# A fourth result buffer, a reordered row of N and a VectorE subtraction in a conditioned residual kernel

## The chip, the cores and the metric

The kernel runs on one core of a Trainium2 chip. The metric is the device time of one execution in microseconds (us). The kernel before took 302.66 us as the median of three runs (299.89 to 302.8). Times inside an execution come from one profiled execution and count from its first instruction.

The core's engines have short names in the profile: PE is TensorE (matrix products; PEld its weight loads), DVE is VectorE (elementwise work of one or two tensors), ACT is ScalarE (copies, casts, functions), POOL is GpSimd (here it issues transfers and little else), SP is SyncE (issues transfers). Products are summed in PSUM, in banks of 128 partitions x 512 fp32 numbers. Everything else lies in SBUF.

## The reference

For each of 8 batches there are an x of 1024 x 512 and a row of condition of 512 numbers. Cut to what matters:

```python
ae  = layernorm(cond) * ln_g + ln_b
xw  = gelu(ae @ w1 + b1) @ w2 + b2            # 2 * 512 * 8 numbers a batch
a, t = split(xw)                               # each 512 x 8
x   = x + (x + x @ (base + a @ t.T))
ys  = cond / sqrt(512)
d   = rsqrt((ys * ys) @ (weight * weight) + 1e-8)
out = x + ((x * ys) @ weight) * d
```

Both layers are linear in x once the condition is known. So out = x P, with P = (2I + base + a t^T) N and N = I + diag(ys) weight diag(d), all 512 x 512 and different for each batch.

## The kernel before, in words

**Numbers.** An fp32 matrix is held as two parts of the type fp32r: an upper part, rounded by an ACT cast, and a lower part, the matrix minus its upper part, mostly by one DVE tensor_sub. A product takes three matmuls: upper times upper, upper times lower and lower times upper. In the names, an h marks an upper and an l a lower part: `nh`/`nl` for N, `ph`/`pl` for P, `sh`/`sl` and `th`/`tl` for sums of blocks. `xs[b, j]` holds both parts of a quarter of x of batch b, `[:, 0]` the upper, `[:, 1]` the lower.

**The setup (to about 80 us).** It computes the condition's network (bank `px` gathers the product with w2, whose 16 blocks are loaded one after another by `w2_group`), then Q = (2I + base) N for the first batches, and the two stacks a and t of low rank, from which each batch gets its term. Batches 2 and 3 are made together by `Pair(2)`, called `two`, which forms Q of both by seven block products instead of eight. For product p, `make_n(p)` makes two rows of blocks of N, `round(p)` forms the sum that the product needs and starts its cast to `nh`, `finish(p)` gives the lower part `nl`, and `unit()` runs half of a product on PE (`pp` in the profile). Inside `n_half` (L335) DVE runs a scalar_tensor_tensor for each of two rows (kk = 0, 1) and then an add of the identity's blocks.

The stack t is made by the generator `rank_t` (L454), one step for each `next(steps)`. The step at L485 multiplies by a selection on PE (bank `ps_t`) and has ACT cast the upper part (`work`). The next step takes the lower part, `st_t`, on DVE, and sends it to memory on POOL's queue (`kept_t`). A later step runs `stack` again for the second group of batches, into another bank `ps_t`. These banks come from `misc`, a PSUM pool with two buffers; the second `ps_t` gets the buffer of the first when `st_t` has read it.

The order of the setup is written out by hand: every DVE, ACT, SP and PE instruction there is pinned to program order. The lines around the change are L811 to L880. After the second `make_n` there, in this order: `round(6)`, two seeds of banks for batch 0 (`seed_first`), half a product, `finish(6)`, `round(3)`, the second stack of t, two w2 blocks, half a product, `round(7)`, the last w2 block, `with_bias(0)` (DVE writes `xab`; ACT casts it to `work`; DVE forms the remainder `work`), `finish(3)`, two halves of product 6, the first stack of a (`ps_a`) and `finish(7)`.

**The main loop (about 74 to 252 us).** 48 tiles of 128 rows of x, 8 for each of batches 0 to 5. `main(b, t)` sums 12 matmuls of 512 columns in a bank `po`; ACT copies it to `o` and issues the store. Between the tiles stand `load_x` (raw x by SP), `split_x` (L710, the parts of a quarter of x), the rank terms (`pr`, with `fa` and `ft` loaded on POOL's queue) and the pairs of later batches. Here DVE, ACT and POOL are not pinned: a planner sets their order from its own costs, mostly along the program; PE keeps the written order. The lower part of `xs[0, 3]`, the last quarter of x of batch 0, is made in another way than the rest: ACT writes minus the upper part there, and a transfer on POOL's queue adds x from memory onto it.

**The late halves (252 us to the end).** Batches 6 and 7 each have two halves of 512 rows. `Seven.part` (L985) does a half with seven block products, in the order 1, 5, 6, 2, 7, 3, 4, pinned again. Products 1, 6, 7 and 4 sum up in bank `sw`, 5 and 3 in `sz`, 2 in `sv`. In between, ACT and DVE take partial sums out of the banks into the two results of the half: `o1` (products 1, 6, 2, 3) and `o2` (5, 7, 4). A product that adds onto a bank waits until the sum before has been read. Each result is 128 x 1024 numbers; they share the tag `o2`, a set of three buffers. A result is stored when it is whole: o1 after product 3, o2 after product 4. The steps of `make_left` for the next half are done one by one between the products.

Of the kernel before, what the change touches and what calls it, by code (L numbers as in the profile page):

```python
# [7 lines left out]
F32 = mybir.dt.float32  # L8
F32R = mybir.dt.float32r
AF = mybir.ActivationFunctionType  # L10
ALU = mybir.AluOpType
# [3 lines left out]
P = 128  # L15
NB = 8
NT = 1024
D = 512
# [12 lines left out]
def cond_resid_kernel(ctx: ExitStack, tc: tile.TileContext, small, cond, condrows, consts,  # L31
# [10 lines left out]
    nc = tc.nc  # L42
# [21 lines left out]
    ve, se, sy = InOrder(nc.vector), InOrder(nc.scalar), InOrder(nc.sync)  # L64
# [99 lines left out]
    def newton_rsqrt(v, sd, shape, name):  # L164

        r = sp.tile(shape, F32, name=f"r_{name}")
        ve.reciprocal(r, sd)
        t = sp.tile(shape, F32, name=f"t_{name}")
        ve.tensor_mul(t, r, r)
        ve.tensor_mul(t, t, v)  # L170
        ve.tensor_scalar(t, t, -0.5, 1.5, ALU.mult, ALU.add)
        return r, t
# [12 lines left out]
    r, t = newton_rsqrt(ve_l, sd, [NB, 1], "l")  # L185
# [103 lines left out]
    r, t = newton_rsqrt(v, sv, [P, KC, NB], "d")  # L289
# [15 lines left out]
    def work_tile():  # L305
        turns[0] += 1
        return work[:, turns[0] % KC, :]
# [24 lines left out]
            d_all[b + i] = t[:, i, :]  # L332
            nc.gpsimd.dma_start(t[:, i, :], d_out[b + i:b + i + 1, :].to_broadcast([P, D]))

    def n_half(b, j):  # L335

        n = npool.tile([P, 2, D], F32, tag="n", name=f"n_{b}_{j}", bufs=4)
        for kk in range(2):
            k = 2 * j + kk
            ve.scalar_tensor_tensor(n[:, kk, :], w_sb[:, k, :], ysT[:, k, b:b + 1],  # L340
                                           d_all[b], ALU.mult, ALU.mult)
        blk = n.rearrange("p k (c i) -> p (k c) i", i=P)[:, 2 * j:2 * j + 6:5, :]
        ve.tensor_add(blk, blk, ident.unsqueeze(1).to_broadcast([P, 2, P]))
        return n
# [49 lines left out]
    def w2_group():  # L394
        h, r, k = todo.pop(0)
        t = big_tile(f"w2_{h}_{r}_{k}")
        sy.dma_start(t, w2[h, r, k])
        if len(todo) == 15:
            sy.dma_start(cst, consts)
        if len(todo) == 8:  # L400
            sy.dma_start(crow, condrows)
            sy.dma_start(b2r, b2rows)
        if len(todo) == 4:
            b_nat.append(big_tile("b_nat"))
            sy.dma_start(b_nat[0], base)
        for j in range(4):
            mm(px[h][32 * j:32 * j + 32, :], hT[:, k, r, :], t[:, j, :],
               start=(r == 0 and k == 0), stop=(r == 1 and k == KC - 1))
# [45 lines left out]
    def rank_t():  # L454


        xb = with_bias(1)
        by = tmp_tile("by")
        ve.scalar_tensor_tensor(by, crow, SCALE, xb, ALU.mult, ALU.mult)
        hi, s = work_tile(), work_tile()  # L460
        se.copy(hi, by)
        yield
        ve.scalar_tensor_tensor(s, hi.bitcast(F32), neg_u, by, ALU.mult, ALU.add)
        by = s.bitcast(F32)
        yield
        pb = misc.tile([P, KC, P], F32, tag="misc", name="pb")
        for k in range(KC):
            turn(pb[:, k, :], by[:, k * P:(k + 1) * P], ident)
        byT = work_tile().rearrange("p (k c) -> p k c", k=KC)
        se.copy(byT, pb)  # L470
        yield
        pt = misc.tile([P, D], F32, tag="misc", name="pt_t")
        for k in range(KC):
            for i, w in enumerate((wh, wl)):
                mm(pt, byT[:, k, :], w[:, k, :], start=(k == 0 and i == 0),
                   stop=(k == KC - 1 and i == 1))
        t = tmp_tile("t")
        ve.tensor_mul(t, pt, drow)
        ve.scalar_tensor_tensor(t, xb, upper, t, ALU.mult, ALU.add)
        th, tl = work_tile(), work_tile()  # L480
        se.copy(th, t)
        yield
        ve.tensor_sub(tl, t, th.bitcast(F32))
        yield
        done = stack((th, tl), neg_t, "t", 0)  # L485
        yield
        stt[0] = done()
        yield
        late_rows.append(stack((th, tl), neg_t, "t", 1, rows[:, 3, :]))
        yield  # L490
# [39 lines left out]
    fold, pools = {}, {}  # L530
# [53 lines left out]
    class Pair:  # L584
# [31 lines left out]
            ve.tensor_sub(r, a, c)  # L616
            return r

        def make_n(self, p):

            if p in (1, 2, 5, 6):
                key, i, j = {1: ("t", 0, 0), 2: ("21", 0, 1), 5: ("12", 1, 0), 6: ("22", 1, 1)}[p]
                self.n[key] = n_half(self.b + i, j)

        def round(self, p):
            self.rest[p] = round_right(self.sums(p), f"{self.b}_p{p}")
# [83 lines left out]
    def split_x(b, j, part=None):  # L710

        t = raw[b, j // 2][:, :, (j % 2) * 2 * P:(j % 2 + 1) * 2 * P]
        if part != 1:
            xs[b, j] = big.tile([P, 2, KC, 2 * P], F32R, tag="big", name=f"xs_{b}_{j}")
            se.copy(xs[b, j][:, 0], t)
        if part != 0:
            hi, lo = xs[b, j][:, 0], xs[b, j][:, 1]
            if b == 0 and j > 2:
                se.mul(lo, hi.bitcast(F32), -1.0)
                nc.gpsimd.dma_start(lo, x[b, j // 2][:, :, (j % 2) * 2 * P:(j % 2 + 1) * 2 * P],  # L720
                                    accum_op=ALU.add)
            else:
                ve.tensor_sub(lo, t, hi.bitcast(F32))

    def split_first(m):

# [24 lines left out]
    def round1(j):  # L751
        n1[j] = round_right(n1[j], f"1_{j}", False)

    n1[0] = n_half(1, 0)
    round1(0)
    n1[1] = n_half(1, 1)
    keep_first((0, 1))
    round1(1)
# [14 lines left out]
    two = Pair(2)  # L773
# [21 lines left out]
    steps = rank_t()  # L795
# [18 lines left out]
    two.unit()  # L814
    next(steps)
    two.unit()
    two.make_n(6)
    w2_group()
    w2_group()
    next(steps)  # L820
    next(steps)
    two.round(6)
    bank = [px[1], misc.tile([P, D], F32, tag="misc", name="pr_0_1")]
    p_tiles(0)
# [15 lines left out]
    hi = work_tile()  # L840
# [15 lines left out]
    for c in range(KC):  # L856
        rank_first(c, bank[c])
    split_x(0, 0, 0)
    split_first(0)
    for c in range(KC):  # L860
# [6 lines left out]
    for f in held[:2]:  # L867
        f()
    two.finish(4)
    split_x(0, 1)  # L870
    for f in held[2:]:
        f()
# [20 lines left out]
    class Seven:  # L893
# [91 lines left out]
        def part(self, g, steps=(), last=False, then=None):  # L985


            b, bank, steps = self.b, {}, iter(steps)
            o1, o2 = (pools["late"].tile([P, 2, D], F32, tag="o2", name=f"o{i}_{b}_{g}", bufs=3)
                      for i in range(2))  # L990
            for p in self.ORDER:
                key = {5: "z", 3: "z", 2: "v"}.get(p, "w")
                first = p in (1, 5, 2)
                if first:
                    pool, tag = (po, "po") if key == "z" else (acc, "acc")
                    bank[key] = [pool.tile([P, 2, HD], F32, tag=tag, name=f"s{key}{i}_{b}_{g}")
                                 for i in range(2 if key == "w" and last else 1)]
                self.product(g, p, bank[key], first)
                o, cols = {1: (o1, slice(0, HD)), 2: (o1, slice(0, HD)), 3: (o1, slice(HD, D)),
                           6: (o1, slice(HD, D)), 4: (o2, slice(0, HD)), 5: (o2, slice(HD, D)),  # L1000
                           7: (o2, slice(HD, D))}[p]
                for m, u in enumerate(bank[key]):
                    u, to = (u, slice(0, 2)) if len(bank[key]) == 1 else (u[:, 0:1], slice(m, m + 1))
                    if p in (2, 3, 7):
                        ve.tensor_add(o[:, to, cols], u, o[:, to, cols])
                    else:
                        se.copy(o[:, to, cols], u)
                    if last and p in (2, 3, 7, 4):
                        self.store(se if p == 4 else sy, o, g, int(p in (4, 7)), to, cols)
                    elif p in (3, 4):  # L1010
                        self.store(sy, o, g, int(p == 4), to, slice(0, D))
                next(steps, None)
                if p == 7 and then:
                    then()
# [63 lines left out]
    for i in range(TILES):  # L1078
        b, t = divmod(i, NTT)
        if t == 0 and i + NTT < TILES:  # L1080
            p_tiles(b + 1)
        main(b, t)
        if t % 4 == 0 and 0 < i < TILES - 4:
            load_x(*divmod(i // 4 + 1, NHALF))
        if t % 2 == 0 and i + 4 < TILES:
            split_x(*divmod(i // 2 + 2, NTT // 2))
        for f, args in after.get((b, t), ()):
            f(*args)
# [76 lines left out]
```

## Time and profile before

| What | us |
|---|---|
| Median of the three runs | 302.66 |
| The runs | 302.8, 299.89, 302.66 |
| The profiled execution's own time | 300.34 |
| Its span, first to last instruction | 298.6 |
| PE works | 290.2 |
| DVE works | 211.5 |
| ACT works | 162.5 |
| POOL works | 35.0 |
| Chain that ended last: share of PE | 73% |
| Chain that ended last: share of DVE | 11% |
| Chain that ended last: share of transfers | 9% |

The clock that TensorE was granted was full in all of the span (mean 1.000). The transfer engines moved 62.66 MB; they were busiest in the first quarter of the span.

How to read the lines below: a timeline line gives the start in us, the duration in us, the engine, the line of the kernel, the operation, output<-inputs, shape and type, and the number of instructions merged into it. In brackets stands how long the engine was idle before, and what ended it. Engine instructions are recorded by helpers, so nearly all show L62 or L45, and one goes by the names of the tiles. A line of the waits gives who waited for what: us in total, times, longest. A matmul's recorded duration overlaps the next one, so the distance of starts tells more.

### The profile page before, as it was taken

The page shows a single profiled execution, that of the slowest core. Times are in us where ns is not written, and L with a number is a line of the kernel's source. Part 1 is how long each engine was busy: PE and PEld are TensorE (multiplying, and loading weights), DVE is VectorE, ACT ScalarE, POOL GpSimd, SP SyncE. Part 2 cuts the span into 40 slices and gives each one's busy share as a digit, 9 for nine tenths or more (in the row PEclk, how much of TensorE's full clock was granted, in tenths as well). Part 3 has the DMA queues.
Part 4 walks back from the last instruction along what each step waited for, and adds up shares of the span by engine and source line. Part 5 has one row for each costly group of instructions (what it writes and reads, how often), then busy time and mean ns, then how long its engine had stood idle before and what let it go on. Part 6 is the DMA issues. An engine that isn't in the chain of part 4 may idle for free.

```text
span 298.6 us, 4005 instructions
## 1 busy us (share of the span) xinstructions
PE 290.2 (97%) x1489; PEld 224.8 (75%) x1489; DVE 211.5 (71%) x299; ACT 162.5 (54%) x247; POOL 35.0 (12%) x73
## 2 busy tenths in 40 slices
PE   8999999899998999999999999999999999999795
PEld 3665566357876778888887888888778888999794
DVE  3779798998916799915669994436456994579722
ACT  4756164176885674667444645536426662665430
POOL 0011000206524551000004500000000000000000
PEclk9999999999999999999999999999999999999999
DMA  6999999993499685435243741151643993172234
GB/s 212 417 426 420 408 394 385 391 350 99 136 293 333 173 262 160 142 125 178 86 178 114 202 169 73 50 202 37 211 142 142 297 322 120 38 269 79 76 141 143
DMA packets 20052, 62.66 MB, mean 210 GB/s; under 512 B 2736, under 2 KB 4528, under 8 KB 15680
## 3 DMA queue, kind: packets, MB, share of 16 engines
q1 hardware_dynamic: 8816, 43.24, 39.2%
q10 hardware_dynamic: 7200, 12.85, 11.5%
q0 software_dynamic: 4016, 6.31, 8.6%
q8 instruction: 12, 0.20, 0.3%
q14 instruction: 8, 0.07, 0.1%
HBM read 44.55 MB, written 17.84 MB: 209 GB/s over the span
## 4 chain that ended last, share of the span: by engine, by line
PE 73%; DVE 11%; DMA 9%; issue 3%; ACT 3%; ACTq 0%; POOL 0%; POOLq 0%; DVEq 0%
PE po L45 39%; PE pp L45 15%; PE sw L45 6%; DMA xs<-in_x 3%; DVE n L62 3%; PE sz L45 3%; PE pg L45 3%; DMA d<-d_out 2%; PE warm L45 2%; DMA d_out<-drow 2%; DVE nl_p L62 2%; PE sv L45 1%; DMA out<-o 1%; DVE pl L62 1%; PE px L45 1%
## 5 line engine op out<-in xcount | busy, mean ns | idle before, releaser
L45 PE MATMUL po<-ph,xs 128*128 128x512 f32 x384 | 124.2, 392 | 0.8 <-DMA xs<-in_x 0.8
L45 PEld LDWEIGHTS po<-ph,xs 128*128 128x128 f32 x384 | 72.0, 188 | 18.1 <-issue 1.7
L45 PE MATMUL po<-pl,xs 128*128 128x512 f32 x192 | 74.8, 390 | 0.0
L62 ACT COPY o<-po 128x512 f32<-128x512 f32 x48 | 28.1, 585 | 49.6 <-PE po L45 49.5
L45 PEld LDWEIGHTS po<-pl,xs 128*128 128x128 f32 x192 | 36.1, 188 | 7.3
L62 DVE TENSOR_TENSOR nl_p<-n,nh_p 128x1024 fp32r<-128x1024 f32 x21 | 25.5, 1221 | 13.3 <-ACT nh_p L62 13.3
L62 DVE TENSOR_TENSOR xs<-x,xs 128x1024 fp32r<-128x1024 f32 (+1 forms) x24 | 28.0, 1173 | 9.3 <-ACT xs L62 9.3
L62 ACT CAST nh_p<-n 128x1024 fp32r<-128x1024 f32 x21 | 22.1, 1053 | 16.9 <-DVE n L62 16.1
L62 ACT CAST xs<-x 128x1024 fp32r<-128x1024 f32 x24 | 24.9, 1051 | 8.2 <-DMA x<-in_x 7.8
L62 ACT COPY q<-pp 128x512 f32<-128x512 f32 x30 | 17.5, 588 | 12.3 <-PE pp L45 12.2
L538 POOL DMA_DIRECT2D fa<-kept_a x28 | 13.8, 513 | 56.2 <-PE pr L45 54.1
L45 PE MATMUL pp<-nh_p,sh 128*128 128x512 f32 x48 | 19.1, 397 | 0.0
L45 PE MATMUL pp<-nl_p,sh 128*128 128x512 f32 x48 | 18.8, 391 | 0.0
L45 PE MATMUL pp<-nh_p,sl 128*128 128x512 f32 x48 | 18.7, 390 | 0.0
L62 DVE SCALAR_TENSOR_TENSOR n<-w_sb,ysT,d 128x512 f32<-128x512 f32 x24 | 16.9, 744 | 1.8 <-DMA d<-d_out 1.8
L62 DVE TENSOR_TENSOR q<-pr,q 128x512 f32<-128x512 f32 x20 | 12.5, 680 | 7.6 <-PE pr L45 7.6
L62 ACT COPY o<-sw 128x512 f32<-128x512 f32 (+1 forms) x15 | 7.5, 502 | 18.5 <-PE sw L45 13.7
L45 PE MATMUL px<-w,hT 128*32 128x512 f32 x128 | 15.6, 599 | 0.0
L538 POOL DMA_DIRECT2D ft<-kept_t x28 | 13.8, 526 | 12.8 <-DMA kept_t<-st_t 9.5
L62 DVE TENSOR_TENSOR n<-n,n 128x1024 f32<-128x1024 f32 x12 | 14.6, 1219 | 0.1
L45 PE MATMUL pp<-nh_p,bh 128*128 128x512 f32 x36 | 14.4, 399 | 0.0
L62 DVE TENSOR_TENSOR pl<-q,ph 128x1024 fp32r<-128x1024 f32 (+1 forms) x10 | 11.0, 1113 | 4.7 <-ACT ph L62 4.7
(198 smaller groups left out, 512.2 us busy)
## 6 DMA issues: line engine op xcount, KB each, us to landing
w<-in_w SPq DMA_DIRECT2D x16, 1024.0 KB, 9.6
x<-in_x SPq DMA_DIRECT2D x16, 1024.0 KB, 5.5
out<-o ACTq DMA_DIRECT2D x48, 256.0 KB, 2.5
out<-o SPq DMA_DIRECT2D x6, 512.0 KB, 3.5
ft<-kept_t POOLq DMA_DIRECT2D x28, 64.0 KB, 2.2
fa<-kept_a POOLq DMA_DIRECT2D x28, 64.0 KB, 2.5
d<-d_out POOLq DMA_DIRECT2D x6, 256.0 KB, 7.2
w_sb<-in_weight SPq DMA_DIRECT2D x2, 512.0 KB, 5.2
```

Source lines behind the costliest of these rows:

```text
L45: tc.keep_in_program_order(nc.tensor.matmul(*args, **kw))
L62: return lambda *a, **kw: pin(f(*a, **kw)) if InOrder.on else f(*a, **kw)
L538: nc.gpsimd.dma_start(fold[name, b][32 * c:32 * c + 32, :], kept[name, g][32 * i:32 * i + 32, :])
```

## The change

Three edits that are independent of each other.

- `n_half` and `make_n` take a function `between`, which is called after the first row's instruction. The hand-written order calls `make_n(6)` after the step of `rank_t` that runs the first stack of t, and gives it the next step (`st_t` and its transfer) as `between`. So DVE's order from row 0, row 1, add, `st_t` becomes row 0, `st_t`, row 1, add. The order of PE's and ACT's instructions stays.
- `split_x` loses its branch for `xs[0, 3]`: its lower part is a tensor_sub on DVE like the others. ACT's multiplication by -1 and the adding transfer on POOL's queue go.
- The tag `o2` of the late halves gets four buffers in place of three.

```diff
-    def n_half(b, j):
+    def n_half(b, j, between=None):
...
             ve.scalar_tensor_tensor(n[:, kk, :], w_sb[:, k, :], ysT[:, k, b:b + 1],
                                            d_all[b], ALU.mult, ALU.mult)
+            if between and not kk:
+                between()
...
-        def make_n(self, p):
+        def make_n(self, p, between=None):
...
-                self.n[key] = n_half(self.b + i, j)
+                self.n[key] = n_half(self.b + i, j, between)
...
             hi, lo = xs[b, j][:, 0], xs[b, j][:, 1]
-            if b == 0 and j > 2:
-                se.mul(lo, hi.bitcast(F32), -1.0)
-                nc.gpsimd.dma_start(lo, x[b, j // 2][:, :, (j % 2) * 2 * P:(j % 2 + 1) * 2 * P],
-                                    accum_op=ALU.add)
-            else:
-                ve.tensor_sub(lo, t, hi.bitcast(F32))
+            ve.tensor_sub(lo, t, hi.bitcast(F32))
...
     two.unit()
-    two.make_n(6)
     w2_group()
     w2_group()
     next(steps)
-    next(steps)
+    two.make_n(6, lambda: next(steps))
     two.round(6)
...
-            o1, o2 = (pools["late"].tile([P, 2, D], F32, tag="o2", name=f"o{i}_{b}_{g}", bufs=3)
+            o1, o2 = (pools["late"].tile([P, 2, D], F32, tag="o2", name=f"o{i}_{b}_{g}", bufs=4)
                       for i in range(2))
```

## The prediction

> **What bounds the kernel now.** The page's busy times come first. Its columns are busy us, share of the span, instructions.
>
> ```profile
> PE 290.2 (97%) x1489; PEld 224.8 (75%) x1489; DVE 211.5 (71%) x299; ACT 162.5 (54%) x247; POOL 35.0 (12%) x73
> ```
>
> TensorE (PE) works nearly all of the time and the change leaves its 1489 matmuls alone, so it can save only what PE stands still. The waits of PE say where:
>
> ```profile
> PE sw L45 <- ACT o L62: 1.6, 1, 1.6
> PE ps_t L45 <- DVE st_t L62: 1.2, 1, 1.2
> PE warm L45 <- DVE eps_l L62: 1.0, 1, 1.0
> PE po L45 <- DMA xs<-in_x: 0.8, 1, 0.8
> ```
>
> Three waits, one for each part of the change; the fourth is the start. These figures leave out the modelled tail of the matmul before, so I take the loss from the starts in PE's timeline. At their usual pace, matmuls of 512 columns start 0.23 apart and of 256 columns 0.12 apart.
>
> ```profile
> 57.39 0.39 PE L45 MATMUL pp<-nh_p,sl 128*128 128x512 f32 x1
> 58.17 0.74 DVE L62 SCALAR_TENSOR_TENSOR st_t<-work,cst,ps_t 128x512 fp32r<-128x512 f32 x1
> 58.96 0.73 PE L45 MATMUL ps_t<-work,sel 128*128 128x512 f32 x2 [1.18 <-DVE st_t L62]
> ...
> 94.50 0.39 PE L45 MATMUL po<-pl,xs 128*128 128x512 f32 x1
> 95.73 0.73 PE L45 MATMUL po<-ph,xs 128*128 128x512 f32 x2 [0.84 <-DMA xs<-in_x]
> ...
> 278.36 0.28 PE L45 MATMUL sv<-ph,xa 128*128 128x256 f32 x1
> 280.28 0.38 PE L45 MATMUL sw<-th,sh 128*128 128x256 f32 x1 [1.64 <-ACT o L62]
> ```
>
> Lost: 58.96 - 57.62 = 1.34; 95.73 - 94.73 = 1.00, and 0.11 more since the first matmul after a stop takes 0.34 instead of 0.23; 280.28 - 278.48 = 1.80. Together 4.2 us, the ceiling of this change.
>
> The timelines of ScalarE (ACT), GpSimd (POOL) and VectorE (DVE) show what is behind them, and one line that limits the first:
>
> ```profile
> 278.21 0.58 ACT L62 COPY o<-sz 128x512 f32<-128x512 f32 x1 [1.75 <-DMA out<-o]
> ...
> 86.06 1.28 POOL L720 DMA_DIRECT2D xs<-in_x  x1 [6.37 <-ACT xs L62]
> ...
> 64.92 0.62 ACT L62 CAST work<-xab 128x512 fp32r<-128x512 f32 x1 [0.22 <-DVE xab L62]
> 66.25 2.35 DVE L62 TENSOR_TENSOR nl_p<-n,nh_p 128x1024 fp32r<-128x1024 f32 x2
> 67.52 0.50 PE L45 MATMUL pp<-nl_p,sh 128*128 128x512 f32 x1
> ```
>
> [...]
>
> **Part 1: fourth o2 buffer.** Results o1 and o2 of three halves share three buffers: with o1 and o2 of (6, half 1) being stored and o1 of (7, half 0) filled, o2 of (7, half 0) has none until the store issued at 273.92 lands 4.19 later, at 278.11. Behind that copy on ACT stand the cast sh and the copy o<-sw; product 7 on PE adds onto the bank which the latter reads. With a free buffer the copy of sz starts when ACT is done with x (275.84 + 0.62, so 276.4), sh at 276.9 (its sraw ends at 276.48) and o<-sw at 277.8, read out at 278.4. PE wants the bank at 278.48. So 1.80 goes, with 0.1 to spare. Next in line: DVE's add for product 7. DVE: o<-sv 278.74, sl 279.35, add 280.5 to 281.2; product 4 wants that bank at 281.36. It fits by 0.15; if not, some tenths come back. After that the work to the end hangs on PE, as before. **-1.80** (bounds -2.0 and 0).
>
> **Part 3: xs(0,3) by VectorE.** Removed: ACT's multiplication by -1 (84.70, 1.06), the adding load on POOL (1.28 to issue, 9.6 to land), and the 3.4 us for which POOL's next ft load waited for it. Added: one DVE tensor_sub of 1024 elements, 1.22 from the row of xs. Its input is cast by 83.02; DVE ends xs(0,2) at 82.80 and then idles until 89.44 (6.64 us), so the sub takes 83.1 to 84.3 of that idle time and is needed at 94.73. Cost on the path: nothing; without that hole it would be 1.22 on DVE. The raw half of x(0,1) stays 1.3 us longer (to 84.3, not 83.0); the loads that follow (82.20, 87.79) wait for others. PE's wait goes whole: **-1.11** (bounds -1.2 and 0).
>
> **Part 2: st_t between the rows of N.** DVE's order becomes row 0, st_t, row 1, add, sums. No instruction is added. Row 0 starts at 56.39; st_t needs ACT's cast, which ends at 57.05, just when row 0 gives way: st_t runs 57.1 to 57.8 instead of 58.17 to 58.91. The second ps_t starts at 57.87: 1.09 earlier. Its DMA kept_t moves with it; on POOL the two loads of d wait for row 1, 0.7 later (58.8), but d is read next at 101.16. The last w2 block landed at 60.88 and is wanted at 62.0. So far 1.09.
>
> But PE then meets DVE again. The sums (n<-n,n at 58.83) now follow the add directly and start about 0.1 later, so the chain behind them does not move up: nh_p 60.2, nl_p 61.3, n of product 7 62.4 to 63.7. Then xab, which waited 0.63 for PE, runs at 63.6; ACT's cast of it stands behind nh_p of product 7, which cannot start before 63.7, and so goes from 64.92 only to 64.7; the remainder work from 65.58 to 65.4; nl_p of product 3 ends at 67.3 instead of 67.46. PE needs it in the row of 67.52 and had no slack there (0.36 since the start before). So PE is 0.2 earlier from here on. The other 0.9 us turns into new waits before ps_a and the first pp<-nl_p, 65.8 to 67.3. I take **-0.2** (bounds -1.1 and +0.1).
>
> **Sum.** 1.80 + 1.11 + 0.2 = 3.1. The profiled execution took 300.34 with a span of 298.6: 295.5 and 297.2 after. The runs shown are 299.89, 302.66 and 302.8, so 300.34 belongs with the lower. From the upper pair it would be 299.6. I take the lower: two of the three waits end on a transfer, which is what may differ between executions, and they go.
>
> **Rivals.** (a) Above, all three parts as worked out: 297.2 (up to 299.6 if the runs fall like the upper pair); 0.68. (b) The row of 67.52 is no wait, and part 2 passes whole: 4.0 us, 296.3; for it, the gap there is only 0.13 over the pace; against it, nl_p ends 0.06 before; 0.1. (c) The fourth buffer frees the copy but another wait takes its place (DVE's add for product 7, margin 0.15; or the buffer given out is again one in store): only parts 2 and 3 stay, 1.3 us, 299.0 (301.4 from the upper pair); 0.17. Four buffers for the four tiles in use speak against it. (d) Slower: from 80 us on, DVE's order is chosen by a planner, and split_x(0,3) needs its sub started by 93.4. Put behind the adds q<-pr (98.75, 2.48), it would end near 102.4 and PE would wait 7.7 instead of 1.1: 297.2 + 7.7 = 304.9. The idle DVE from 82.80 speaks against it; 0.05.
>
> **Range and chances.** One per cent is 3.0 us, about what a measurement of this kernel can tell from no change. Case (a) is just over that on the smallest reading and 1.8% if the medians fall 302.7 to 297.2. Range 295.6 to 300.2: (a), (b) and the lower half of (c). Faster by over 1%: 0.63, from most of (a) and all of (b); slower 0.05, (d); within 1% the remaining 0.32.
>
> **What would show it.** Of PE's waits, po <- DMA xs and sw <- ACT o gone; ps_t's down to about 0.2 and near 0.9 of new idle time between 65.8 and 67.4, ended by DVE work and nl_p. DVE's xs sub starts between 83 and 85. POOL has 72 instructions, PE still 1489. Wrong if PE shows a wait over 0.5 elsewhere after 70 us, if ACT's copy o<-sz still waits for a store, or if PE's starts at 95 are not 1.3 earlier.

## The result and the profile after

The changed kernel took 297.47 us (median of six runs, 296.81 to 297.7), against 302.12 us (299.89 to 302.8, six runs) for the kernel before. The ratio is 0.9856, with a 95% interval of 0.9821 to 0.9892. The profiled execution took 296.81 us, with a span of 295.0 against 298.6. The prediction was 297.2.

The page first, as for the kernel before:

```profile
PE 289.6 (98%) x1489; PEld 224.6 (76%) x1489; DVE 212.7 (72%) x300; ACT 161.4 (55%) x246; POOL 33.5 (11%) x72
```

PE works as long as before within 0.6 us; DVE has one instruction more, ACT and POOL one fewer each. What went is idle time. The waits of PE:

```profile
PE warm L45 <- DVE eps_l L62: 1.0, 1, 1.0
PE pp L45 <- DVE nl_p L62: 0.4, 1, 0.4
PE ps_a L45 <- DVE work L62: 0.2, 1, 0.2
```

The three waits are gone, and two small ones are new, both in front of the lower part for product 3, where the prediction had put them. PE's timeline at the places of the change and at the two new waits:

```profile
57.57 0.73 PE L45 MATMUL ps_t<-work,sel 128*128 128x512 f32 x2
...
65.93 0.50 PE L45 MATMUL ps_a<-work,sel 128*128 128x512 f32 x1 [0.23 <-DVE work L62]
66.27 0.40 PE L45 MATMUL pp<-nh_p,sh 128*128 128x512 f32 x1
67.07 0.50 PE L45 MATMUL pp<-nl_p,sh 128*128 128x512 f32 x1 [0.40 <-DVE nl_p L62]
...
94.02 0.39 PE L45 MATMUL po<-pl,xs 128*128 128x512 f32 x1
94.24 0.62 PE L45 MATMUL po<-ph,xs 128*128 128x512 f32 x2
...
276.72 0.28 PE L45 MATMUL sv<-ph,xa 128*128 128x256 f32 x1
276.84 0.29 PE L45 MATMUL sw<-th,sh 128*128 128x256 f32 x1
```

PE runs the same 1489 matmuls in the same order in both kernels, so each can be paired with itself. The table gives start after minus start before, in us. "Ahead of it" repeats the value behind the place above, so a drift of at most 0.05 between two places is counted in the lower one:

| Place | ahead of it | behind it | this place gives |
|---|---|---|---|
| start to the first ps_t, nothing changed there | 0 | -0.31 | -0.31 |
| second ps_t | -0.31 | -1.39 | -1.08 |
| ps_a and the two matmuls behind it | -1.39 | -0.45 | +0.94 |
| xs(0,3) | -0.45 | -1.59 | -1.14 |
| product 7 of (7, half 0) | -1.59 | -3.53 | -1.94 |

What stands behind these steps, in ACT's and DVE's timelines:

```profile
56.77 0.75 DVE L62 SCALAR_TENSOR_TENSOR st_t<-work,cst,ps_t 128x512 fp32r<-128x512 f32 x1
64.48 0.61 ACT L62 CAST work<-xab 128x512 fp32r<-128x512 f32 x1
65.79 2.35 DVE L62 TENSOR_TENSOR nl_p<-n,nh_p 128x1024 fp32r<-128x1024 f32 x2
...
274.15 0.62 ACT L62 CAST x<-x 128x512 fp32r<-128x512 f32 x1
274.67 0.59 ACT L62 COPY o<-sz 128x512 f32<-128x512 f32 x1
...
82.60 1.23 DVE L62 TENSOR_TENSOR xs<-x,xs 128x1024 fp32r<-128x1024 f32 x1 [0.25 <-ACT xs L62]
88.62 1.23 DVE L62 TENSOR_TENSOR xs<-x,xs 128x1024 fp32r<-128x1024 f32 x1 [4.79 <-ACT xs L62]
```

Against the kernel before, and less the 0.31 from the start, st_t is 1.09 us earlier, but ACT's cast of xab only 0.13 and nl_p 0.15. The copy o<-sz follows the cast of x without a wait. The subtraction that is new starts at 82.60, in the hole that DVE had, and the hole stays 4.79 us wide.

### The profile page after: what moved, and what is told of

Its sections match the earlier page's. It is cut to its first block, busy times and chain, and to the rows that moved or that the text cites. A ratio compares the mean times of both kernels' runs of the same rounds, so it can differ in the third digit from the quotient of the medians.

```text
span 295.0 us, 3996 instructions
## 1 busy us (share of the span) xinstructions
PE 289.6 (98%) x1489; PEld 224.6 (76%) x1489; DVE 212.7 (72%) x300; ACT 161.4 (55%) x246; POOL 33.5 (11%) x72
## 4 chain that ended last, share of the span: by engine, by line
PE 80%; DVE 9%; DMA 6%; ACT 3%; issue 1%; SPq 0%; ACTq 0%
PE po L45 45%; PE pp L45 16%; PE sw L45 7%; PE sz L45 4%; DVE n L62 4%; PE pg L45 3%; DMA d<-d_out 2%; DVE nl_p L62 2%; PE sv L45 2%; DMA d_out<-drow 2%; DMA w_sb<-in_weight 1%; PE pr L45 1%; ACT work L62 1%; DVE work L62 1%; DVE sl L62 1%
## 5 line engine op out<-in xcount | busy, mean ns | idle before, releaser
L62 DVE TENSOR_TENSOR xs<-x,xs 128x1024 fp32r<-128x1024 f32 (+1 forms) x25 | 29.4, 1178 | 13.4 <-ACT xs L62 13.4
```

The costliest lines, as they stand in the source:

```text
L62: return lambda *a, **kw: pin(f(*a, **kw)) if InOrder.on else f(*a, **kw)
```

## The experiments

### Each part alone

The fourth buffer alone (`bufs=3` to `bufs=4`):

> The kernel before with the fourth o2 buffer alone. If each part takes away its own wait of TensorE: the copy o<-sz no longer waits for a store, sw's wait of 1.8 us goes, the waits at ps_t (1.3) and at po for the adding load (1.1) stay; the span falls from 298.6 by 1.8 to 296.8, and the median by about 1.8. The runs of the kernel before lie 2.9 us apart and those of the changed kernel 0.9. If it is the store of a late half whose length differs between executions, the runs come together here; if it is the adding load, they stay 2 to 3 us apart. Rival: another wait (VectorE's add for product 7) takes the place of the store's, and less than 0.5 us is gained.

299.12 us, runs 297.7 to 301.6. The ratio to the kernel before, run beside it, is 0.9945 (95% interval 0.9923 to 0.9968; so in all that follow). The wait of sw is gone: PE came 1.8 us closer at that place. The runs did not come together, so the store is not what spreads them; its wait does vary, from 1.1 to 1.8 us in the eight profiles with three buffers. In its profiled execution the adding load took 10.4 us, and PE waited longer for it than in the kernel before:

```profile
94.75 0.39 PE L45 MATMUL po<-pl,xs 128*128 128x512 f32 x1
96.76 0.73 PE L45 MATMUL po<-ph,xs 128*128 128x512 f32 x2 [1.62 <-DMA xs<-in_x]
```

The reordering alone:

```diff
+            if between and not kk:
+                between()
...
-    two.make_n(6)
     w2_group()
     w2_group()
     next(steps)
-    next(steps)
+    two.make_n(6, lambda: next(steps))
```

> The kernel before with st_t between the rows of N alone. If TensorE meets VectorE's chain again at ps_a and the first pp<-nl_p of product 3: 1.1 us earlier at the second ps_t, 0.15 us (0 to 0.3) earlier from 67 us on, and then the wait at 95.7 for the adding load takes that back, if the load does not start earlier, so the median is the same within 0.3 us. Rival: what is gained at ps_t is kept, 1.1 us less.

300.56 us, ratio 0.9968 (0.9949 to 0.9987). That is 1.0 us less by the ratio and 0.5 by the medians, more than expected. In the profiled execution PE did as expected up to 67 us: 1.10 earlier at the second ps_t, then 0.93 back, 0.17 in all. But it did not wait at 95 at all, since the adding load took only 7.2 us. That execution, at 298.73 us, is the shortest of the 22 runs and doesn't stand for the rest. Whether the reordering shortens that load is taken up below.

The subtraction alone:

```diff
-            if b == 0 and j > 2:
-                se.mul(lo, hi.bitcast(F32), -1.0)
...
-            else:
-                ve.tensor_sub(lo, t, hi.bitcast(F32))
+            ve.tensor_sub(lo, t, hi.bitcast(F32))
```

> The kernel before with the lower part of xs(0,3) by VectorE alone. If each part takes away its own wait: po's wait at 95 us goes, the two others stay, span 298.6 - 1.1 = 297.5. If the adding load's length is what makes runs of the kernel before differ (299.9 to 302.8), then the median falls by more than in the profiled execution, about 2.5 us, and the runs come within 1 us of each other. If the spread has another source, the median falls by 1.1 us and the runs stay 2 to 3 us apart.

299.05 us, ratio 0.9953 (0.9936 to 0.9969). That is 1.4 us (0.9 to 1.9); the median is 2.0 below that of the runs beside it (301.08). The 19 runs lie 1.4 us apart. Of 58 runs of the kernel before, 54 lie 4.2 us apart (299.0 to 303.2), and four go up to 305.2. PE's wait for xs is gone, the two others stay. So the adding load is the main source of the spread. The medians say that on average it costs more than the 1.11 us of the one profiled execution; the ratio leaves that open, since its interval takes in 1.11.

### The adding load, and what its length costs

The adding load made a plain one:

```diff
-                nc.gpsimd.dma_start(lo, x[b, j // 2][:, :, (j % 2) * 2 * P:(j % 2 + 1) * 2 * P],
-                                    accum_op=ALU.add)
+                nc.gpsimd.dma_start(lo, x[b, j // 2][:, :, (j % 2) * 2 * P:(j % 2 + 1) * 2 * P])
```

> The kernel before with the transfer for xs(0,3) made plain: it overwrites instead of adding, so the lower part of that quarter is wrong (it holds x itself). Everything else, the multiplication by -1 and POOL's order too, stays. If the adding makes it long (7.2 to 10.4 us in the profiles so far), a plain transfer of the same bytes lands in about 4 us or less and TensorE does not wait at 95; if the traffic beside it does (a load of x, fa and ft loads and stores), it lands in 7 to 10 us as before.

It landed 5.3 us after its issue, and PE did not wait; 299.36 us, ratio 0.9937 (0.9917 to 0.9958). The load of x(1, half 1) issued in its midst took 8.9 us (8.0 in the kernel before), so that load was no quicker than before. The result lies between the two expectations, of which the 4 us was the author's estimate (the stores of 512 KB by SP in the kernel before took 3.5 us in the median). The adding has a share: against 7.2 to 11.3 us for the adding form, a plain transfer of the same bytes takes 5.3 in this place, in one profile, and 18 of the 20 runs lie between 298.2 and 299.8, like those of the subtraction alone. One of the other two took 303.93, so the adding is not all that can lengthen a run. The share of the traffic shows only on its neighbour: the same load of x took 7.5 to 8.0 us beside the adding load, and 5.4 and 5.6 where the transfer for xs(0,3) is gone (changed kernel, subtraction alone). No run shows the load without traffic beside it, so how much of its own length the traffic makes stays open.

Four more profiles, two of the kernel before and two of the reordering alone:

> The kernel before, for one more profile of its adding load (9.6 us, and 10.4 us with the fourth buffer alone, in the profiles so far). If the reordering shortens that load by moving the ft and fa loads ahead, this shows 9 us or more and an idle TensorE at 95; if its length only varies, anything from 7 to 10.5.

> The kernel before once more, as above: 9 us or more if the reordering is what shortens the load, 7 to 10.5 if it only varies.

> The kernel before with the reordering in N alone, for one more profile of its adding load (7.2 us in the profile so far). If the reordering shortens the load, 8 us or less and no wait at 95; if its length only varies, anything from 7 to 10.5.

> The reordering alone once more, as above: 8 us or less if the reordering shortens the load, 7 to 10.5 if it only varies.

| Kernel | adding load, us | PE's wait for it, us | this execution, us |
|---|---|---|---|
| before | 9.6 | 0.8 | 300.34 |
| before, first again | 11.3 | 2.5 | 303.14 |
| before, second again | 9.6 | 0.8 | 300.15 |
| buffer alone | 10.4 | 1.6 | 299.58 |
| reordering alone | 7.2 | 0 | 298.73 |
| reordering, first again | 7.8 | 0 | 299.48 |
| reordering, second again | 10.2 | 1.4 | 301.48 |

The load's length varies by 4 us over the seven: 9.6 to 11.3 in the kernel before, 7.2 to 10.2 with the reordering. The shorter ones come with the reordering, but 10.2 does too, so an effect of the reordering on it stays open. The execution at 303.14 shows a second cost. First PE's timeline of it, then the table by stage (length; busy us and count for PE, PEld, DVE, ACT and POOL; PE's granted clock; DMA share; GB/s):

```profile
94.63 0.39 PE L45 MATMUL po<-pl,xs 128*128 128x512 f32 x1
97.49 0.72 PE L45 MATMUL po<-ph,xs 128*128 128x512 f32 x2 [2.47 <-DMA xs<-in_x]
```

```profile
94.00:98.00 4.00, 1.53 (x7) 0.99 (x6) 1.81 (x2) 0.96 (x2) 0.27 (x1) 1.00 1.04 331
98.00:102.00 4.00, 4.00 (x14) 2.39 (x13) 0.00 (x0) 0.58 (x1) 0.22 (x1) 0.57 0.13 34
102.00:106.00 4.00, 4.00 (x22) 3.31 (x19) 3.95 (x7) 3.23 (x6) 3.59 (x8) 1.00 0.51 148
```

The two starts are 2.86 apart, a stop of 2.6 us. Behind it PE's granted clock is 0.57 on average from 98 to 102. At the 0.50 that shorter stretches show in a run below, that is an estimated 4 x (1 - 0.57) / 0.5 = 3.4 us at half clock. Against the first profile of the kernel before its matmuls are 1.76 us late when the load lands and 3.29 when the clock is back: 1.5 us more, which no list of waits shows. In this execution the adding load cost 2.6 + 0.1 + 1.5 = 4.2 us, and not 1.11.

The clock of the other runs fits. One such stretch in 300 us makes a mean clock of about 1 - 0.5 x 3.4 / 300 = 0.994. Of the 85 runs of the kernel before that stood beside the experiments, 14 have 0.994 or less, all at 301.9 us or more. None of the 43 runs of four kernels without the adding load has (the changed one, the same without the reordering, the subtraction alone, and the last one below), nor any of the 22 of the reordering alone, which speaks for an effect of it on the load without settling it.

### The reordering, and the chain that took it back

The changed kernel without the reordering (fourth buffer and subtraction alone):

> The changed kernel without the reordering in N: the fourth buffer and the subtraction alone. If the reordering nets 0.15 us (TensorE 1.08 earlier at the second ps_t, 0.94 of it given back at ps_a and pp<-nl_p), this takes 0.15 us more than the changed kernel run beside it, about 297.6, and has the 1.2 us wait at ps_t and none at ps_a. Rival: the reordering is worth what it saves at ps_t, and this takes 1.1 us more.

297.72 us, ratio 0.9897 (0.9861 to 0.9933). PE's wait of 1.2 at ps_t is there, and none at ps_a or nl_p, as expected.

The changed kernel once more, on the same chip:

> The changed kernel, unchanged, to be compared on the same chip with the three beside it: 297.5, its runs within 1.5 us of each other, no run with a mean granted clock of 0.994 or less.

297.54 us (297.05 to 297.67), ratio 0.9886 (0.985 to 0.9921). The reordering is worth 0.18 us by the medians; the intervals do not tell that from nothing. The profile of this execution gives 1.08 gained at ps_t and 0.94 lost again, as the first one did.

If DVE's chain through the sum for product 7 takes it back, moving that sum should free it. First try, behind the lower part for product 3:

```diff
     two.unit()
-    two.round(7)
     w2_group()
...
     xa = (s,)
     two.finish(3)
+    two.round(7)
     two.units(2)
```

> The changed kernel with the sum and cast for product 7 moved behind the remainder of xab and the lower part for product 3. If VectorE's chain through that sum is what gives back 0.9 us of the reordering (0.39 before ps_a, 0.57 before the first pp<-nl_p of product 3), both waits shrink to below 0.1 us each and the execution is 0.7 to 0.9 us shorter than the changed kernel: span 294.2, about 296.7. Rival: the sum for product 7 is not what holds xab's remainder and nl_p, and the waits stay: 297.5. Second rival: product 7 is now late itself, a new wait at its first matmul of up to 1 us.

299.71 us, ratio 0.9956 (0.9929 to 0.9984): 2.2 us above the 297.5 of the changed kernel, where 0.8 less had been expected. The waits at ps_a and nl_p went, but ACT's cast for product 7 now stands ahead of its cast of ps_a, and st_a is late:

```profile
69.87 0.39 PE L45 MATMUL pp<-nh_p,sl 128*128 128x512 f32 x1
71.96 0.49 PE L45 MATMUL px<-st_t,st_a 32*128 32x512 f32 x1 [1.70 <-DVE st_a L62]
```

The table by stage again, and PE at three starts:

```profile
73.00:73.50 0.50, 0.50 (x3) 0.34 (x3) 0.50 (x2) 0.50 (x3) 0.16 (x1) 1.00 0.37 86
73.50:74.00 0.50, 0.50 (x3) 0.44 (x2) 0.50 (x2) 0.50 (x3) 0.00 (x0) 0.72 0.78 234
74.00:76.00 2.00, 2.00 (x6) 1.54 (x5) 2.00 (x4) 0.96 (x3) 0.75 (x2) 0.50 0.28 84
76.00:77.00 1.00, 1.00 (x3) 0.78 (x3) 1.00 (x2) 0.67 (x2) 1.00 (x3) 0.50 0.33 78
77.00:77.50 0.50, 0.50 (x3) 0.39 (x2) 0.50 (x2) 0.00 (x0) 0.50 (x2) 0.87 0.71 139
77.50:78.00 0.50, 0.50 (x3) 0.40 (x3) 0.50 (x2) 0.01 (x1) 0.50 (x2) 1.00 0.61 143
```

```profile
75.36 0.63 PE L45 MATMUL ps_a<-work,sel 128*128 128x512 f32 x1
75.78 0.63 PE L45 MATMUL pp<-nh_p,sh 128*128 128x512 f32 x1
76.21 0.63 PE L45 MATMUL pp<-nl_p,sh 128*128 128x512 f32 x1
```

Two starts are 0.43 apart where 0.23 is usual: the half clock again (0.50 from 74 to 77), here from about 73.7 to 77.1 by the means of 0.72 and 0.87 at its two ends. The late st_a cost 1.8 us and the clock 1.6. The slow clock comes in some executions only. Eight of the 14 runs have a mean clock of 0.994 or less and take 299.57 to 301.69 us; the six at 0.998 or more take 298.12 to 298.64. The slow stretch lasts 3.4 us, as long as the estimate for the execution at 303.14, and the stop ahead of it is shorter (starts 2.09 apart, 2.86 there).

Second try, behind the stack of a, with product 7's lower part behind st_a:

```diff
     done = stack(xa, neg_a, "a", 0)
-    two.finish(7)
+    two.round(7)
     sa[0] = done()
...
     seed_first(3, bank[3])
+    two.finish(7)
```

> The changed kernel with the sum and the cast for product 7 moved behind the first stack of a, and its lower part behind st_a and the last seed. In the kernel with the sum moved less far the waits at ps_a and pp<-nl_p went (0.88 us back), but st_a came 1.7 us late behind product 7's cast and lower part. If that order was all that was wrong, st_a is in time here, no wait over 0.2 us is left between 57 and 80 us, and it is 0.7 to 0.9 us shorter than the changed kernel beside it. Rival: VectorE is full from 61 to 75 us in any order, and as much is lost at px<-st_a or at the first product 7 matmuls.

296.82 us (296.41 to 297.17), ratio 0.9865 (0.9826 to 0.9904): 0.72 below the changed kernel beside it by the medians; of the six runs each, only those between 297.05 and 297.17 overlap. PE's waits in the profile are down to the one at the start:

```profile
PE warm L45 <- DVE eps_l L62: 1.0, 1, 1.0
```

Here PE gains 1.08 at the second ps_t and 0.80 of it is left at the main loop's tiles (1.18 earlier than in the kernel before, then 0.90, with 0.10 of both from the start); the rest goes in steps of about 0.1 that no wait names. So the chain through the sum for product 7 is shown to be what took most of the gain back. This is the fastest version of the study.

## Why the prediction was right

**Bound and ceiling.** Right. PE's matmuls did not change and the gain is what it stopped waiting. The losses read from the starts (1.34, 1.11, 1.80) hold better than the list of waits, which has 1.2, 0.8 and 1.6.

**Fourth buffer, -1.80.** Right: -1.94 in the changed kernel, -1.8 alone. The rival that another wait takes its place fell: DVE's add for product 7 was in time. The stop for want of a buffer came once in the span; the cause, too few buffers, was the one named. The 1.80, too, is one execution's figure: the list has 1.6 for it, in a range of 1.1 to 1.8.

**Subtraction, -1.11.** The mechanism was right, and in the paired profile it gave 1.14. As a figure for the median it was probably too small (2.0 by the medians of the subtraction alone, 1.4 by the ratio). What the adding load costs differs between executions: 1.1 to 4.2 us in three profiles of the kernel before, and nothing in two with the reordering. I took the one length at hand. This term is the likely reason why the median fell by 3.6 us when measured again, and not by 3.1. The 4.65 of the first runs holds another 1.0 that the change does not account for: the six runs of the kernel before lay high (302.12, against 301.1 in 58 and in 27 later ones). The half clock behind a long stop was in no step.

**Reordering, -0.2.** Right, with the place and the size of what comes back: 1.08 forward (1.09 predicted), 0.94 back (0.9), 0.14 kept. The rival that it passes whole fell with the changed kernel's own profile.

**Sum and median.** 3.1 for the profiled execution; measured 3.53, of which 0.31 arose ahead of anything that was changed, so 3.22; the second profile of the changed kernel gives 3.15 in the same way. Choosing the lower group of runs was right for the reason given: a wait that differs between executions went. Of the two named, only the adding load's is shown to spread the runs. Taking 3.1 off the profiled execution, and not off the median, matched each loss with the execution that it was read from. That the figure came within 0.3 us of the median is in part luck, since the start alone shifts an execution by some tenths (0.31 earlier in one profile of the changed kernel, 0.42 later in the other).

**The slower rival** (a planner that puts the new subtraction late) did not happen: the subtraction ran at 82.60, more than ten microseconds ahead of its use. It had been put between 83 and 85; PE and all that hangs on it ran 0.45 us earlier there. Its price was not tried.

## What to carry to other kernels

Pair each matmul of the bounding engine with itself in both traces: the steps in the difference show what every edit gave, and where it was taken back. Before trusting a gain ahead of a hand-written order, find the next place at which the two engines meet, and ask what the other engine does until there: 1.1 us shrank to 0.14 until that chain was reordered too. A wait that ends on a transfer is worth its average over executions (here 0 to 2.5 us in seven profiles), so look at the spread of the runs, and at their mean clocks, before taking its size from one profile.

## What had not been expected of the hardware

Two stops of PE (starts 2.09 and 2.86 us apart) were each followed by about 3.4 us at half clock (0.50 from 74 to 77 behind the first, a mean of 0.57 from 98 to 102 behind the second), which cost 1.6 and 1.5 us more. It isn't a matter of the length alone. In the kernel with the subtraction alone two starts were 2.12 apart, at the wait of sw, and the mean clock of that execution was 1.000:

```profile
277.53 0.28 PE L45 MATMUL sv<-ph,xa 128*128 128x256 f32 x1
279.65 0.38 PE L45 MATMUL sw<-th,sh 128*128 128x256 f32 x1 [1.84 <-ACT o L62]
```

Nor did the clock fall behind two other stops: at sw in the kernel before (starts 1.92 apart, clock 1.00 from 279 to 287) and at the adding load with the buffer alone (2.01 apart, 1.00 from 96 to 104). What sets these three apart from the stop of 2.09 is open.

The adding transfer of 0.5 MB took 7.2 to 11.3 us in seven profiles, and the same transfer without the addition 5.3 us in one, with the same load of x beside it.
